# First slots of a sandwich kernel reordered: weight low parts on TensorE, second block from slot 1, third from slot 10

## Chip, cores and metric

The kernel runs on one core of a Trainium2 chip. Its time is the device time of one execution in microseconds (us): before the change the median of three runs is 1156.1 us (1156.03 to 1156.17). Where and why time goes is read from one execution that the hardware profiler recorded.

A core has five engines with a queue of instructions each, worked in order: TensorE (PE; PEld is its weight load), VectorE (DVE), ScalarE (ACT), GpSimd (POOL) and SyncE (SP), which issues nearly all of this kernel's DMAs.

## What is computed

The input is 16 sequences of 512 rows of 128 values (D = 128). Two layers follow, each with layer norms around it and an addition of its input:

```python
x = x + layernorm(attn(layernorm(x)))
x = x + layernorm(ffn(layernorm(x)))

# attn: a diagonal recurrence with 64 states, done in the reference by FFT
h = real(ifft(fft(kernel) * fft(u @ B_w.T)))
y = h @ C_w.T + D * u

# ffn: 8 experts, all of them computed, H = 128, F = 512
router_probs = softmax(x @ w_router)
gate_weights = softmax(x @ w_gating / 0.1)
g = x @ w_gate[e];  up = x @ w_up[e]
expert_out[e] = (silu(g) * up) @ w_down[e]
cw = router_probs * gate_weights
cw = cw / (sum(cw) + 1e-9)
out = sum over e of expert_out[e] * cw[e]
```

## The kernel before

**Tiling.** A block is one sequence of 512 rows (T = 512), kept with features on the 128 partitions. There are 16 blocks. A block's expert layer is 32 slots: 8 experts times 4 pieces of 128 of the 512 hidden values. Slot n makes `g` and `u` (`up`, L564 for the silu), and the piece of slot n - 4 (`LAG`) is multiplied into the expert's output (`down`). Four pieces add up in one PSUM bank, which `combine` weights with the row's `cw` and adds to the block's `acc`.

**Precision.** A float32 product is made of three products of a shorter type: `mm3` (L338, L339, L340) multiplies high by high, the weight's low part by the high part, and the weight's high part by the low part. Each weight and each moving operand so exists as a high part (a copy by ScalarE) and a low part (the difference). A weight number k is expert k // 3, and gate, up or down by k % 3. `split_w` makes the high part on ScalarE (L110) and the low part on GpSimd (L115). For the first three weights (`AHEAD`), `rest` (L682, L683) makes the difference on TensorE, as identity times the weight plus minus identity times the high part, each float32 product in two records of the profile, and ScalarE copies the result (L684).

**Slots.** The last loop writes all queues in one fixed order, slot by slot. In a slot n it emits: the high part of slot n - 1 (`split_hi`, L580, ScalarE), the six products and the silu of slot n, the down products of slot n - 4, every fourth slot `combine`, then one weight split where one is due (`n % 4 < 3`), then steps of the side work, then the low part of slot n - 1 (`split_lo`, L586, on VectorE or GpSimd) and the gate product of slot n (`gate`, L575, VectorE). Whether VectorE or GpSimd makes a low part (`lo_pool`) is decided from `busy`, three planned loads.

**Side work.** `front`, `route` and `back` are generators: everything that a block needs before its slots (layer norm, recurrence, residual, layer norm, router) and after them. Each `yield` gives a smallest distance in slots and the planned cost on VectorE, ScalarE and GpSimd; `steps` takes a step where the plan has room. `chain(b)` is `front` and `route` of block b. Chain 1 begins in slot 0, chain 2 in slot 4, chain i in slot 32 i - 67. Inside `front`, `ln_coef` makes variances on VectorE (`ve`, L281), GpSimd raises them to the power -1/2 (`rs`, L283), VectorE makes the shift (`nm`, L286). `ln_add` adds the residual (L302).

**Block 0.** Its front is written out ahead of the loop: VectorE makes the recurrence's table and state, TensorE takes state and projection (L698, L675), `residual` adds the input and takes statistics (L729), `norm` normalizes on ScalarE and VectorE (L514, L516), TensorE transposes (L752), ScalarE copies to `xh` and `xT` (L755, L756), VectorE makes `xl` (L757). `keep_warm` (L736) issues products whose result nobody reads: 9, 4 and 0 of them (`WARM`). The router's exponentials of block 0 are on ScalarE (L428, L429); those of later blocks are eight powers on GpSimd (L433).

**Buffers.** `g` has two PSUM banks and `u` three: g(n) waits for the silu of slot n - 2, and u(n) for the last reader of u(n - 3), which is `lo` where VectorE makes it and the gate product where GpSimd does. The first eight weights (`OWN`) are loaded into the rings `hi` and `lo` of the slots (five each, two of `lo` being scratch of block 0); later ones go into a ring of five, and the split of one starts the load of the fifth after it.

Of the kernel before, what the change touches and what calls it, by code (L numbers as in the profile page):

```python
# [11 lines left out]
F32 = mybir.dt.float32  # L12
F32R = mybir.dt.float32r
# [6 lines left out]
P = 128  # L20
# [6 lines left out]
NF = F // P  # L27
LAG = 4
LEAD = 67
OWN = 8  # L30
WARM = 9, 4, 0
AHEAD = 3
LN_EPS = 1e-5


# [12 lines left out]
def sandwich(ctx, tc, x, a_params, B_w, C_w, Dv, w_router, w_gating, w_gate, w_up, w_down, sines, out):  # L48
# [31 lines left out]
            nc.sync.dma_start(out=xts[b][:, k], in_=x[b].rearrange("(c p) d -> p c d", p=P)[:, k])  # L80


    spare = [hp.tile([P, F], F32R, name=f"spare{i}", tag="lo", bufs=LAG + 1).bitcast(F32) for i in range(2)]

# [51 lines left out]
    dbc = const.tile([P, D], F32, name="dbc")  # L136
    for k in range(AHEAD, OWN):
        load_w(k)
        if k == 4 and NB > 1:
            load_x(1)  # L140
            nc.sync.dma_start(out=dbc, in_=Dv.partition_broadcast(P))

# [25 lines left out]
    def bank(pl, tag, name):  # L168
        return pl.tile([P, T], F32, name=name, tag=tag)
# [176 lines left out]
    def front(b):  # L346
# [58 lines left out]
        vec.tensor_tensor(xl, xT, xh.bitcast(F32), ALU.subtract)  # L405
        blocks[b] = dict(xh=xh, xl=xl, x2=x2, xT=xT)

    def route(b):

        G2 = NT * 2  # L410
        xT = blocks[b]["xT"]
        yield 1, 0, 0, 0, "f"
        lg = ps_f.tile([P, G2, E], F32, name=f"lg{b}", tag="f")
        for c in range(NT):
            pe.matmul(  # L415
                lg[:, 2 * c : 2 * c + 2], xT[:, P * c : P * c + P], wrg.rearrange("d g e -> d (g e)"),
                start=True, stop=True,
            )
        yield 1, 0.4, 0, 0
        bc = lambda t, n: t.unsqueeze(2).broadcast_to([P, n, E])  # L420
        mx = small.tile([P, G2], F32, name="mx", bufs=2)
        vec.tensor_reduce(mx, lg, AX.X, ALU.max)
        ez = small.tile([P, G2, E], F32, name="ez", bufs=2)
        vec.tensor_tensor(ez, lg, bc(mx, G2), ALU.subtract)
        own[0] = False
        if b == 0:
            e4 = ez.rearrange("p (c g) e -> p c g e", g=2)
            act.activation(e4[:, :, 0], e4[:, :, 0], AF.Exp)  # L428
            act.activation(e4[:, :, 1], e4[:, :, 1], AF.Exp, scale=10.0)  # L429
        else:  # L430
            for i in range(G2):
                yield 1, 0, 0, 1.62
                gp.tensor_tensor(ez[:, i], bases.rearrange("p c g e -> p (c g) e")[:, i], ez[:, i], ALU.pow)  # L433
        yield 2, 0.65, 0, 0
        sm = small.tile([P, G2], F32, name="sm", bufs=2)
        vec.tensor_reduce(sm, ez, AX.X, ALU.add)
        vec.reciprocal(sm, sm)
        vec.tensor_tensor(ez, ez, bc(sm, G2), ALU.mult)
        yield 1, 0.75, 0, 0
        pr = ez.rearrange("p (c g) e -> p c g e", g=2)  # L440
        cw0 = small.tile([P, NT, E], F32, name="cw0", bufs=2)
# [78 lines left out]
    def halves(t):  # L520
        return [[t[:, 2 * h], t[:, 2 * h + 1]] for h in range(2)]
# [110 lines left out]
    def turn(k):  # L632
        for _ in range(k):
            next(rot, None)
# [60 lines left out]
    def state(c):  # L695
        k = quarter[c]
        vec.tensor_tensor(vm[:, k], v[:, k], tre[:, k], ALU.mult)
        pe.matmul(yps[c], vm[:, k], cT, start=False, stop=True)  # L698

    vec.tensor_tensor(v[:, left], bus[0], tre[:, left], ALU.mult)  # L700
    turn(2)
    scan(left, 0.0)
    turn(2)
    state(0)
    state(1)
    turn(2)
    vec.tensor_tensor(v[:, right], bus[1], tre[:, right], ALU.mult)
    lo0 = rest(0, ps_u, "u")
    lo0()
    scan(right, v[:, 2 * P - 1 : 2 * P])  # L710
    stat(0, yps[0])
    stat(1, yps[1])
    state(2)
    state(3)
    rest(1, ps_g, "g")()
    r0 = rstd(s6s[0])
    stat(2, yps[2])
    stat(3, yps[3])
    r1 = rstd(s6s[1])
    rest(2, ps_f, "f")()  # L720

# [10 lines left out]
    warm = bank(ps_g, "g", "warm")  # L732

    def keep_warm(k):
        for _ in range(k):
            pe.matmul(warm, W[0, 0][0][:, :P], W[0, 0][0], start=True, stop=True)  # L736

    keep_warm(WARM[0])
    residual(0, r0[1])
    q0 = rstd(s6s[0])  # L740
    residual(1, r1[1])
# [3 lines left out]
    xh = fe.tile([D, T], F32R, name="xh0", tag="xh", bufs=2)  # L745
    xl = fe.tile([D, T], F32R, name="xl0", tag="xl", bufs=2)
    xT = work("ft_x0")
    for h, q in enumerate((q0, q1)):
        norm(halves(xn)[h], halves(x2)[h], q[1], shift(*q), True)
        ps = bank(ps_u, "u", f"xT0{h}")[:, : 2 * P]  # L750
        for i in range(2):
            pe.transpose(ps[:, P * i : P * i + P], xn[:, 2 * h + i], ident)  # L752
        keep_warm(WARM[1 + h])
        k = slice(2 * P * h, 2 * P * h + 2 * P)
        act.copy(xh[:, k], ps)  # L755
        act.copy(xT[:, k], ps)  # L756
        vec.tensor_tensor(xl[:, k], ps, xh[:, k].bitcast(F32), ALU.subtract)  # L757
    for h, r in enumerate((r0, r1)):
        vec.scalar_tensor_tensor(x2m[:, 2 * h : 2 * h + 2], r[0][:, :, 0], -1.0, r[1], ALU.mult, ALU.mult)
    blocks[0] = dict(xh=xh, xl=xl, x2=x2, xT=xT, x2m=x2m)  # L760
    first_route = route(0)

    def first():
# [43 lines left out]
    for n in range(total + LAG):  # L807
# [8 lines left out]
        if n < total:  # L816
            up(n, *[first] * (n == 0))
        if n == 0:
            begin(n, 0, first_route, 1, routed)
            if NB > 1:  # L820
                begin(n, 1, chain(1), 1)
        if n == 3:
            act.copy(bT[0], bT32)
            gp.tensor_tensor(bT[1], bT32, bT[0].bitcast(F32), ALU.subtract)
        for i in range(NB):
            if i > 1 and n == max(4, 32 * i - LEAD):
                begin(n, i, chain(i))
        m = n - LAG
        if 0 <= m < total:
# [2 lines left out]
        if m >= 0 and m % 4 == 3:  # L832
            take((0.6, 0, 1.23), (9, 9, 9))
            combine(m // 32, m // 4 % 8)
            if m % 32 == 31 and m // 32 in accs:
                begin(n, m // 32 + 0.5, back(m // 32, accs.pop(m // 32)))
        if nsplit < 3 * E and n < total and n % 4 < 3:
            take((0, 0.5, 1.23), (9, 9, 9))
            split_next(1)
        if n < total:  # L840
# [1 line left out]
        if 0 <= n - 1 < total:  # L842
            split_lo(n - 1)
        if n < total:
            lo_pool[n] = busy[2] < busy[0] and n < total - 3
            gate(n)


# [25 lines left out]
```

## Time and profile before

| | before |
|---|---|
| median of 3 runs | 1156.1 us (1156.03 to 1156.17) |
| profiled execution's own time | 1155.96 us |
| its span, first to last instruction | 1154.1 us |
| granted TensorE clock, mean | 0.997 |
| busy: PE, DVE, ACT, POOL | 1131.5, 922.9, 698.1, 745.6 us |
| first gate product starts | 26.41 us |

In a row of the order of time, the columns are: start in us, duration in us, engine, line, operation, output <- inputs, shapes, how many, and in brackets the engine's idle time before it and what ended it. Products of TensorE overlap: one takes 0.40 us, but the next starts 0.23 us after it. A busy TensorE is therefore not always TensorE at its fastest. In a table of stretches each engine's busy time stands with its number of instructions, and after them the clock that TensorE was granted (1.00 is full speed).

### The profile page before, as it was taken

The numbers are of one execution on the slowest core, as the hardware profiler recorded it, in microseconds if no ns is written. First come the engines' busy times: TensorE is split into PE (matmuls) and PEld (weight loads), VectorE is DVE, ScalarE is ACT, GpSimd is POOL, SyncE is SP. The second block draws the span as 40 slices with busy tenths as digits, with TensorE's granted clock in tenths as the row PEclk, the third lists the DMA queues.
The fourth block names the chain that finished last, engine by engine and source line by source line (L and its number), as shares of the span: only waits on it lengthen the run. The fifth ranks groups of instructions, "written<-read, shape, count | busy, mean of one in ns | idle before, by whom it ended". The sixth has DMA issues, their size and how long they took to land.

```text
span 1154.1 us, 16183 instructions
## 1 busy us (share of the span) xinstructions
PE 1131.5 (98%) x4978; PEld 913.3 (79%) x4978; DVE 922.9 (80%) x2101; ACT 698.1 (60%) x1348; POOL 745.6 (65%) x570
## 2 busy tenths in 40 slices
PE   6899999999999999999999999999999999999997
PEld 4678788888888888888888888888888888888885
DVE  6888888887878878787887878888787887868666
ACT  3766656656566655656566565655657566565564
POOL 1679576776757766585866748577585856647442
PEclk9999999999999999999999999999999999999999
DMA  4140312203122131302212130130302202111120
GB/s 152 50 149 4 93 55 56 92 29 92 47 65 64 38 96 43 92 28 74 73 38 83 38 109 29 56 90 30 92 29 81 66 19 74 47 56 28 31 71 10
DMA packets 65894, 71.23 MB, mean 62 GB/s; under 512 B 8624, under 2 KB 50320, under 8 KB 65808
## 3 DMA queue, kind: packets, MB, share of 16 engines
q1 hardware_dynamic: 65392, 70.04, 20.0%
q8 instruction: 39, 0.64, 0.2%
q14 instruction: 47, 0.39, 0.1%
q10 hardware_dynamic: 416, 0.16, 0.1%
HBM read 54.98 MB, written 15.20 MB: 61 GB/s over the span
## 4 chain that ended last, share of the span: by engine, by line
PE 90%; DVE 4%; POOL 3%; issue 2%; ACT 0%; DMA 0%; DVEq 0%; POOLq 0%
PE g L338 10%; PE d L338 10%; PE g L340 10%; PE d L339 10%; PE uu L338 10%; PE d L340 10%; PE uu L340 10%; PE g L339 10%; PE uu L339 9%; PE yp L387 1%; POOL ez L433 1%; PE lg L415 1%; DVE x L302 0%; POOL acc L609 0%; DVE lo L586 0%
## 5 line engine op out<-in xcount | busy, mean ns | idle before, releaser
L586 POOL TENSOR_TENSOR lo<-hh,hi 128x512 fp32r<-128x512 f32 x196 | 261.9, 1336 | 155.1 <-ACT hi L580 155.0
L580 ACT CAST hi<-uu 128x512 fp32r<-128x512 f32 x316 | 185.4, 587 | 244.4 <-DVE uu L575 235.9
L564 ACT ACTIVATE sg<-g 128x512 f32<-128x512 f32 x512 | 306.7, 599 | 17.5 <-PE g L340 11.7
L575 DVE TENSOR_TENSOR uu<-sg,uu 128x512 f32<-128x512 f32 x316 | 218.7, 692 | 93.9 <-ACT sg L564 83.3
L586 DVE TENSOR_TENSOR lo<-uu,hi 128x512 fp32r<-128x512 f32 x316 | 216.9, 687 | 95.9 <-ACT hi L580 93.2
L609 POOL TENSOR_TENSOR acc<-acc,ct 128x512 f32<-128x512 f32 x109 | 142.4, 1306 | 138.9 <-DVE ct L606 89.7
L580 ACT CAST hi<-hh 128x512 fp32r<-128x512 f32 x196 | 121.6, 621 | 162.5 <-DVE hh L575 160.7
L338 PE MATMUL g<-xh,wgh 128*128 128x512 f32 x512 | 206.8, 404 | 2.4 <-ACT sg L564 1.8
L338 PE MATMUL uu<-xh,wuh 128*128 128x512 f32 x512 | 203.9, 398 | 4.3 <-DVE lo L586 4.3
L339 PE MATMUL d<-hi,wdl 128*128 128x512 f32 x512 | 203.3, 397 | 0.0
L340 PE MATMUL g<-xl,wgh 128*128 128x512 f32 x512 | 203.1, 397 | 0.0
L338 PE MATMUL d<-hi,wdh 128*128 128x512 f32 x512 | 203.0, 396 | 0.0
L340 PE MATMUL uu<-xl,wuh 128*128 128x512 f32 x512 | 201.4, 393 | 0.0
L340 PE MATMUL d<-lo,wdh 128*128 128x512 f32 x512 | 201.1, 393 | 0.0
L339 PE MATMUL g<-xh,wgl 128*128 128x512 f32 x512 | 200.8, 392 | 0.0
L339 PE MATMUL uu<-xh,wul 128*128 128x512 f32 x512 | 198.6, 388 | 0.0
L433 POOL TENSOR_TENSOR ez<-bases,ez 128x8 f32<-128x8 f32 x120 | 195.7, 1650 | 0.0
L575 DVE TENSOR_TENSOR hh<-sg,uu 128x512 f32<-128x512 f32 x196 | 133.5, 681 | 12.5 <-ACT sg L564 5.1
L338 PEld LDWEIGHTS g<-xh,wgh 128*128 128x128 f32 x512 | 96.1, 188 | 27.7 <-ACT sg L564 5.2
L338 PEld LDWEIGHTS uu<-xh,wuh 128*128 128x128 f32 x512 | 95.9, 187 | 27.8 <-DVE lo L586 6.0
L339 PEld LDWEIGHTS uu<-xh,wul 128*128 128x128 f32 x512 | 96.4, 188 | 23.8 <-POOL wul L115 0.2
L340 PEld LDWEIGHTS d<-lo,wdh 128*128 128x128 f32 x512 | 96.8, 189 | 22.9
(172 smaller groups left out, 1336.8 us busy)
## 6 DMA issues: line engine op xcount, KB each, us to landing
cwb<-scw SPq DMA_DIRECT2D x64, 512.0 KB
xt<-in_L_attn_u_dram SPq DMA_DIRECT2D x15, 256.0 KB
sco<-ob SPq DMA_DIRECT2D x60, 64.0 KB
ot<-sco SPq DMA_DIRECT2D x15, 256.0 KB
out_dram<-x SPq DMA_DIRECT2D x15, 256.0 KB
scr_u<-blk_u SPq DMA_DIRECT2D x52, 64.0 KB
ft_u<-scr_u SPq DMA_DIRECT2D x13, 256.0 KB
scr_x<-blk_x SPq DMA_DIRECT2D x52, 64.0 KB
```

The costliest lines, as they stand in the source:

```text
L338: pe.matmul(ps, w[0][:, cs], mh, start=first, stop=False)
L339: pe.matmul(ps, w[1][:, cs], mh, start=False, stop=False)
L340: pe.matmul(ps, w[0][:, cs], ml, start=False, stop=last)
L387: pe.matmul(yp[:, c], v[:, P * c : P * c + P], cT, start=True, stop=True)
L415: pe.matmul(lg[:, 2 * c : 2 * c + 2], xT[:, P * c : P * c + P], wrg.rearrange("d g e -> d (g e)"), start=True, stop=True,)
L433: gp.tensor_tensor(ez[:, i], bases.rearrange("p c g e -> p (c g) e")[:, i], ez[:, i], ALU.pow)
L564: act.activation(s, g, AF.Silu)
L575: vec.tensor_tensor(h, s, u, ALU.mult)
L580: act.copy(hi, pend[n])
L586: (gp if lo_pool[n] else vec).tensor_tensor(lo, h, hi.bitcast(F32), ALU.subtract)
L609: add = lambda: eng.tensor_tensor(acc, acc, t, ALU.add)
```

## The change

- Four weights instead of three are split by `rest`, their copies from PSUM all come at the end, and the products of the first stand ahead of the first pair of state products. Weight 3 is loaded earlier; seven weights instead of eight lie in the slots' rings, and a third scratch tile is set aside in the ring `lo`.
- The warming products are gone.
- The last normalization of block 0 is on VectorE alone, in four operations that subtract and multiply; both halves' `xl` come after both transposes. Half of the router's products stand ahead of the first gate products.
- Chain 1 begins in slot 1 and the rest of block 0's routing in slot 1 as well; chain 2 begins in slot 10. Weight splits begin in slot 3 with weight 4. In slots 0 to 3 no low part is on GpSimd.
- Block 1's exponentials are on ScalarE too, as a step with a planned cost of 1.6.

```diff
-OWN = 8
-WARM = 9, 4, 0
-AHEAD = 3
+OWN = 7
+AHEAD = 4
...
-    spare = [hp.tile([P, F], F32R, name=f"spare{i}", tag="lo", bufs=LAG + 1).bitcast(F32) for i in range(2)]
+    spare = [hp.tile([P, F], F32R, name=f"spare{i}", tag="lo", bufs=LAG + 1).bitcast(F32) for i in range(3)]
...
-        if k == 4 and NB > 1:
+        if k == OWN - 1 and NB > 1:
             load_x(1)
...
+    def logits(b):
+        return ps_f.tile([P, NT * 2, E], F32, name=f"lg{b}", tag="f")
+
+    def score(lg, xT, cs):
+        for c in cs:
             pe.matmul(
                 lg[:, 2 * c : 2 * c + 2], xT[:, P * c : P * c + P], wrg.rearrange("d g e -> d (g e)"),
                 start=True, stop=True,
             )
+
+    def route(b):
...
+        if b > 0:
+            lg = logits(b)
+            score(lg, xT, range(NT))
+        else:
+            lg = blocks[0]["lg"]
+            score(lg, xT, (2, 3))
...
-        if b == 0:
+        if b <= 1:
+            if b == 1:
+                yield 1, 0, 1.6, 0
             e4 = ez.rearrange("p (c g) e -> p c g e", g=2)
             act.activation(e4[:, :, 0], e4[:, :, 0], AF.Exp)
...
     vec.tensor_tensor(v[:, left], bus[0], tre[:, left], ALU.mult)
+    lo = [rest(0, ps_u, "u")]
     turn(2)
     scan(left, 0.0)
     turn(2)
     state(0)
     state(1)
+    lo.append(rest(1, ps_f, "f"))
     turn(2)
     vec.tensor_tensor(v[:, right], bus[1], tre[:, right], ALU.mult)
-    lo0 = rest(0, ps_u, "u")
-    lo0()
     scan(right, v[:, 2 * P - 1 : 2 * P])
     stat(0, yps[0])
     stat(1, yps[1])
     state(2)
     state(3)
-    rest(1, ps_g, "g")()
+    lo.append(rest(2, ps_g, "g"))
     r0 = rstd(s6s[0])
     stat(2, yps[2])
     stat(3, yps[3])
     r1 = rstd(s6s[1])
-    rest(2, ps_f, "f")()
+    lo.append(rest(3, ps_g, "g"))
+    for f in lo:
+        f()
...
-    keep_warm(WARM[0])
     residual(0, r0[1])
...
-    for h, q in enumerate((q0, q1)):
-        norm(halves(xn)[h], halves(x2)[h], q[1], shift(*q), True)
+    xps = []
+    lg = logits(0)
+    for h, (mv, rs) in enumerate((q0, q1)):
         ps = bank(ps_u, "u", f"xT0{h}")[:, : 2 * P]
+        xps.append(ps)
         for i in range(2):
-            pe.transpose(ps[:, P * i : P * i + P], xn[:, 2 * h + i], ident)
-        keep_warm(WARM[1 + h])
-        k = slice(2 * P * h, 2 * P * h + 2 * P)
-        act.copy(xh[:, k], ps)
-        act.copy(xT[:, k], ps)
-        vec.tensor_tensor(xl[:, k], ps, xh[:, k].bitcast(F32), ALU.subtract)
+            c = 2 * h + i
+            vec.tensor_scalar(xn[:, c], x2[:, c], mv[:, i, 0:1], rs[:, i : i + 1], ALU.subtract, ALU.mult)
+            pe.transpose(ps[:, P * i : P * i + P], xn[:, c], ident)
+        act.copy(xh[:, (left, right)[h]], ps)
+        act.copy(xT[:, (left, right)[h]], ps)
+    for h, k in enumerate((left, right)):
+        vec.tensor_tensor(xl[:, k], xps[h], xh[:, k].bitcast(F32), ALU.subtract)
+    score(lg, xT, (0, 1))
...
         if n == 0:
-            begin(n, 0, first_route, 1, routed)
-            if NB > 1:
-                begin(n, 1, chain(1), 1)
-        if n == 3:
+            begin(n + 1, 0, first_route, 1, routed)
+        if n == 1 and NB > 1:
+            begin(n, 1, chain(1), 1)
+        if n == 4:
             act.copy(bT[0], bT32)
             gp.tensor_tensor(bT[1], bT32, bT[0].bitcast(F32), ALU.subtract)
         for i in range(NB):
-            if i > 1 and n == max(4, 32 * i - LEAD):
+            if i > 1 and n == max(10, 32 * i - LEAD):
                 begin(n, i, chain(i))
...
-        if nsplit < 3 * E and n < total and n % 4 < 3:
+        if nsplit < 3 * E and n < total and (n == 3 or n > 3 and n % 4 < 3):
             take((0, 0.5, 1.23), (9, 9, 9))
             split_next(1)
...
-            lo_pool[n] = busy[2] < busy[0] and n < total - 3
+            lo_pool[n] = busy[2] < busy[0] and 4 <= n < total - 3
             gate(n)
```

More of the change, by code (lines that the diff above doesn't have):

```diff
@@ L406, in front @@
         blocks[b] = dict(xh=xh, xl=xl, x2=x2, xT=xT)
+    def logits(b):
+        return ps_f.tile([P, NT * 2, E], F32, name=f"lg{b}", tag="f")
+    def score(lg, xT, cs):
+        for c in cs:
+            pe.matmul(
+                lg[:, 2 * c : 2 * c + 2], xT[:, P * c : P * c + P], wrg.rearrange("d g e -> d (g e)"),
+                start=True, stop=True,
+            )
     def route(b):
@@ L412, in route @@
         yield 1, 0, 0, 0, "f"
[L413 to L418, printed above, removed]
+        if b > 0:
[4 more added lines that the diff above has]
+            score(lg, xT, (2, 3))
         yield 1, 0.4, 0, 0
@@ L730, in residual @@
             stat(c, x2[:, c])
[L732 to L736, printed above, removed]
-    keep_warm(WARM[0])
     residual(0, r0[1])
@@ L747, in sandwich @@
     xT = work("ft_x0")
-    for h, q in enumerate((q0, q1)):
-        norm(halves(xn)[h], halves(x2)[h], q[1], shift(*q), True)
+    xps = []
+    lg = logits(0)
+    for h, (mv, rs) in enumerate((q0, q1)):
         ps = bank(ps_u, "u", f"xT0{h}")[:, : 2 * P]
+        xps.append(ps)
         for i in range(2):
-            pe.transpose(ps[:, P * i : P * i + P], xn[:, 2 * h + i], ident)
-        keep_warm(WARM[1 + h])
-        k = slice(2 * P * h, 2 * P * h + 2 * P)
-        act.copy(xh[:, k], ps)
-        act.copy(xT[:, k], ps)
-        vec.tensor_tensor(xl[:, k], ps, xh[:, k].bitcast(F32), ALU.subtract)
-    for h, r in enumerate((r0, r1)):
-        vec.scalar_tensor_tensor(x2m[:, 2 * h : 2 * h + 2], r[0][:, :, 0], -1.0, r[1], ALU.mult, ALU.mult)
-    blocks[0] = dict(xh=xh, xl=xl, x2=x2, xT=xT, x2m=x2m)
+            c = 2 * h + i
[6 more added lines that the diff above has]
+    score(lg, xT, (0, 1))
+    for h, (mv, rs) in enumerate((r0, r1)):
+        vec.scalar_tensor_tensor(x2m[:, 2 * h : 2 * h + 2], mv[:, :, 0], -1.0, rs, ALU.mult, ALU.mult)
+    blocks[0] = dict(xh=xh, xl=xl, x2=x2, xT=xT, x2m=x2m, lg=lg)
     first_route = route(0)
```

## Prediction

> **Names.** Block 0 is worked in 32 slots. Slot n issues three gate products g(n), three up products uu(n) and, from slot 4 on, three down products d(n-4); ScalarE makes the silu sg(n) and the high part hi(n), VectorE the gate product and mostly the low part lo(n). S(n) is the start of g(n) on TensorE. Weight number k is expert k/3; k mod 3 = 0, 1, 2 is gate, up, down (wg, wu, wd).
>
> **What bounds the kernel now.** I read the stretches first. The columns are: stretch, its length, busy time of PE, PEld, DVE, ACT, POOL, granted clock, DMA share, GB/s.
>
> ```profile
> 20.00:24.00 4.00, 3.69 (x15) 2.73 (x16) 1.64 (x8) 1.48 (x4) 1.20 (x2) 1.00 0.22 66
> 24.00:28.00 4.00, 2.67 (x14) 1.50 (x12) 1.40 (x6) 1.55 (x5) 0.00 (x0) 1.00 0.00 0
> 26.40:46.40 20.00, 16.94 (x73) 12.20 (x74) 14.86 (x44) 14.75 (x31) 10.71 (x10) 1.00 0.09 28
> 46.40:80.00 33.60, 31.06 (x129) 24.08 (x128) 29.02 (x55) 22.01 (x46) 25.11 (x20) 0.95 0.43 127
> 80.00:124.00 44.00, 43.16 (x196) 34.73 (x195) 36.85 (x79) 27.87 (x54) 35.55 (x27) 1.00 0.07 24
> 124.00:1100.00 976.00, 975.88 (x4325) 794.35 (x4326) 787.73 (x1728) 596.10 (x1150) 647.99 (x481) 1.00 0.20 61
> ```
>
> From 124 us on TensorE is busy in 975.88 of 976.00 us; slots follow each other at 2.085 us (9 products of 0.2315). Nothing that is only rearranged can win there. All that can move lies ahead of 124: the time to the first product (26.41), and two holes, which the order of time shows.
>
> ```profile
> 34.96 1.01 POOL L283 TENSOR_TENSOR rs<-ve,neghalf 128x4 f32<-128x4 f32 x1
> 35.94 1.27 POOL L586 TENSOR_TENSOR lo<-hh,hi 128x512 fp32r<-128x512 f32 x1
> 36.01 1.22 DVE L286 SCALAR_TENSOR_TENSOR nm<-mv,rs 128x4 f32<-128x4 f32 x1
> 37.15 0.68 DVE L586 TENSOR_TENSOR lo<-uu,hi 128x512 fp32r<-128x512 f32 x1
> 37.88 0.50 PE L338 MATMUL uu<-xh,wuh 128*128 128x512 f32 x1 [1.88 <-DVE lo L586]
> ...
> 64.65 1.31 POOL L115 TENSOR_TENSOR wul<-raw,wuh 128x512 fp32r<-128x512 f32 x1
> 66.12 0.40 PE L339 MATMUL uu<-xh,wul 128*128 128x512 f32 x1
> ...
> 71.20 3.19 DVE L302 SCALAR_TENSOR_TENSOR x<-du,rs,xt 128x128 f32<-128x128 f32 x4
> 71.43 1.28 POOL L609 TENSOR_TENSOR acc<-acc,ct 128x512 f32<-128x512 f32 x1 [0.71 <-DVE ct L606]
> 72.68 1.31 POOL L115 TENSOR_TENSOR wul<-raw,wuh 128x512 fp32r<-128x512 f32 x1
> 74.32 0.68 DVE L586 TENSOR_TENSOR lo<-uu,hi 128x512 fp32r<-128x512 f32 x1
> 75.05 0.79 PE L338 MATMUL uu<-xh,wuh 128*128 128x512 f32 x1 [2.17 <-DVE lo L586]
> ```
>
> The reader is to see one mechanism twice. A small VectorE operation on SBUF operands (nm takes 0.15 us elsewhere) ends only when GpSimd's running operation ends (36.01 + 1.22 = 37.23, GpSimd's 35.94 + 1.27 = 37.21). Behind it in VectorE's queue stands lo, which frees the PSUM bank that uu three slots later needs. At 71.20 four such operations stood against two GpSimd operations in a row. After the second hole, products were 0.43 apart instead of 0.23 until 77.8 (granted clock 0.50 there). The middle pair is the third thing to see: the low part of expert 4's up weight ends at 65.96, and its reader starts at 66.12. There was no slack.
>
> Prices from S(n): S17 = 67.27 to S21 = 80.02 is 12.75, where four slots take 8.34: 4.4 us lost. Slot 13 lost 0.4 (58.62), slot 40 lost 0.9 (123.86). The last hole starts at slot 4.
>
> **Part 1, the way to the first product.** The x2 of the second half still needs the same VectorE chain, whose last variance ends at 21.32. After it stand today: a wait for nine warming products (20.87 to 23.50) ahead of the transposes, ScalarE's queue, and a shift coefficient at 24.78 queued behind xl, which waited 2.7 us for ScalarE. After the change the four normalizations are all on VectorE (0.35 us, some 0.23 apart) and no warming stands before the transposes. Against it: the low parts on TensorE (four passes, 0.43 apart, 1.72 us each) now stand one ahead of each pair of y products. The first starts at 13.3 and its y pair at 15.0 (was 14.00, hidden under the scan, which ends at 16.05); the second moves the other y pair from 16.69 to 17.24, and the statistics wait for it: +0.5. The chain: variance 21.8, GpSimd's power 0.70 to 22.6, last two normalizations to 23.2, transposes to 23.65, xh 23.7, first product 0.42 later as today (25.99 to 26.41): 24.1. Today it is 26.41. The third product waits for xl until 24.7 (today 27.15), and only half of the router's products stand before uu(0) (four of 0.10): uu(0) at 25.4 against 28.29: **-2.9**.
>
> Here a rule speaks against the change. "TensorE: Matmul & The Clock Gate" in the Trainium skill (Part 1: The HAM clock gate) says that the clock is halved after an idle window of about 3.4 us; the warming products kept TensorE busy. The row: 1.88 us idle before 37.88 cost no clock, 2.17 before 75.05 halved it for 2.7 us, which is earlier than a full window. Without warming, the fourth low part ends at 21.4 and gaps of 0.8, 0.5 and less follow. By the row, nothing; if the clock fell anyway, the six products up to uu(0) would cost 0.2 more each, with the router some 1.0, partly hidden under the table load. I take 0.
>
> **Part 2, slots 0 to 4.** silu, gate, high part, silu is one chain: 30.66, 31.29, 32.01, 32.54, so 1.88 a slot, more than six products (1.39). It stays. The three weight splits (ScalarE 0.5, GpSimd 1.3 each) go from slots 0 to 2, and with them the hold on VectorE; VectorE gets all of lo instead (0.62 a slot). Chain: table load ends 27.75, sg(0) 27.8, sg(1) 29.65, sg(2) 31.7, sg(3) 33.7. But weight 4 (wu of expert 1) is now split in slot 3: its ScalarE half stands behind sg(3) (34.2 to 34.8), GpSimd's ends at 36.1, and uu(4)'s second product reads it: 36.2. Behind it wait uu(4), d(0) and lo(3), which takes the buffer that d(0) frees. Today that product is at 38.22. Up to S8 both then run almost dense: 43.95 against 46.38: **-2.4**. The route arithmetic (1.6 us of VectorE) and coefficients of block 1 run in the time when GpSimd is empty.
>
> **Part 3, slots 8 to 25.** Until S12 nothing is late (S12 = 53.0, was 55.42). The splits are one slot later against their use: before, slot 12 split weights 12, 13, 14 in slots 12, 13, 14; now it is 11, 12, 13 in slots 12, 13, 14, and 12 and 13 are read in slot 16 as before. In GpSimd's queue six operations stand from slot 12 to the low part of 13 (wd 11, rs, lo, acc, wg 12, wu 13: 5 x 1.26 + 1.0 = 7.3), where four stood (60.89 to 65.96). VectorE waits in slot 10 for bu (about 50.75), so gates are 4 us behind TensorE, as today; sg(12) comes at 56.4, weight 11's split at 57.5, weight 13's low part at 65.0. uu(16) wants it at S12 + 8.34 + 0.81 (y products) + 0.93 = 63.1: **+2.0**. S17 = 66.3 (67.27).
> Slot 16: rs stands behind weight 14's low part and ends at 68.5; nm waits for it, then for lo (69.85): VectorE loses 2.9 us as at 67.27 to 69.48 today. The residual (two and two now, not four) then meets weight 16's low part until 74.9; lo(17) ends at 76.0; uu(20) starts there, against 73.8: with small waits for sg, +3.0 for slots 19 to 21. S21 = 77.8 (80.02): **-2.2**.
> Slots 20 to 24 repeat it: sg(20) at 79.3, weight 17's low part to 81.7, rs 82.7, lo 84.0, nm then; uu(23) waits from 82.7 for lo(20), 84.9: +2.2; weight 19's low part ends at 88.6, uu(24) wanted it at 87.6: +1.1. S25 = 89.9, where today it is 89.50 less 0.70 for the block 2 product that is not yet issued: 88.8. **+1.1**. Slot 28 has wd 20, ul, acc, wg 21, wu 22 and no lag left: nothing. The SP queue is no part of this: weight 3, loaded earlier, is needed at 12, x of block 1 at 29.
>
> **Part 4, block 1's exponentials.** Eight GpSimd powers (8 x 1.65 = 13.2 us) go, off the path as TensorE was full at 98 to 117. ScalarE gets two exponentials and two table loads between sg(29) and sg(30). The row for a load:
>
> ```profile
> 29.14 0.21 ACT L429 ACTIVATE ez<-ez 128x32 f32<-128x32 f32 x1
> 29.36 1.28 ACT L564 ACT_TABLE_LOAD   x1
> 30.66 0.60 ACT L564 ACTIVATE sg<-g 128x512 f32<-128x512 f32 x1
> ```
>
> "ScalarE: Activation LUTs" (What ACT_TABLE_LOAD costs) gives 1283 ns for the load and some 1380 ns more to drain, 2.66 for a switch. The row shows 1.28 and the silu 0.02 after it: no second part. By the row sg(30) is 2 x 1.28 + 0.4 = 3.0 late, and g(32), two slots on, allows about 3.0: **+0.3** (0 to 0.6). By the page it would be 5.7 late: +2.7. I take the row. The late hole of slot 40 may go with the powers or stay: **-0.4**. The third block from slot 10 instead of 4 only frees VectorE early; its end, slot 64, is far.
>
> **Sum.** +1.1 + 0.3 - 0.4 = +1.0 on the profiled execution's own 1155.96: 1157.0; the median lies 0.1 above it: **1157.1**. So 2.4 won at the head is given back between slots 16 and 25, while the old hole of 4.4 reappears as smaller ones.
>
> **Rivals.** (a) The holes don't come back. For it: a residual in pairs gives lo its turn; three splits are gone from slots 0 to 2; nm at 48.98 passed in 0.15 when GpSimd was idle. Against: three of four nm here stood 1.2 us. Then -2.4 - 4.8 and up to 2.5 for the late weights: 1149 to 1152.5, about 1151. (b) Slower: the half clock. Two holes of part 3 last 1.9 and 2.2 us, at the edge of the 1.88 that did nothing and the 2.17 that halved it; the price at 75.05 was six products of 0.2 plus the change over, 1.3 to 1.4. It decides from one such hole (1158.5); with both, 1159.9. (c) The order does nothing to the head: if the first product waits for something not seen, part 1's 2.9 is less; it would need ScalarE's four low-part copies (last to 22.05) to hold xh at 22.8. Unlikely; 1158 to 1159, counted with (b).
>
> **Numbers.** A measurement of this kernel can tell about 0.2% (2.3 us) from no change: 1153.8 to 1158.4. Forecast 0.48 (own range 1154 to 1159: faster 0.02, same 0.38, slower 0.08); (a) 0.23 (faster 0.20, same 0.03); (b) and (c) 0.29 (same 0.04, slower 0.25). Together faster 0.22, same 0.45, slower 0.33. Range 1151 to 1160.5: the likely part of (a) below, both half clocks above.
>
> **To check in the profile of the changed kernel.** First product at 24.1 and uu(0) at 25.4 (part 1; half clock there would show in products 0.43 apart); uu(4)'s second product at 36.2 released by GpSimd's wul (part 2); S8 at 44, S12 at 53; a wait of uu(16) on wul near 63 to 65, nm of about 1.2 us ahead of lo, waits at uu(20), uu(23), uu(24) (part 3); two loads of 1.28 and g(32) at most a little late (part 4). It would be wrong if those waits are absent, if they come with a clock of 0.5, or if slots after 32 open.

## The result: slower by 12.6 us

The changed kernel takes 1168.73 us (median; 1168.47 to 1169.02), the kernel before 1156.13 us: 1.0106 of it, with a 95% interval of 1.0088 to 1.0123. The forecast was 1157.1, and its range ended at 1160.5. Its profiled execution has a span of 1167.1 us (1154.1 before).

The stretches of the changed kernel come first, with the columns of the prediction's first view (stretch, length, busy time of PE, PEld, DVE, ACT and POOL, granted clock, DMA share, GB/s).

```profile
24.00:28.00 4.00, 3.96 (x15) 3.10 (x15) 1.35 (x6) 1.29 (x5) 0.00 (x0) 0.60 0.00 1
34.00:38.00 4.00, 1.64 (x6) 0.81 (x5) 3.39 (x13) 3.40 (x8) 1.29 (x1) 1.00 0.00 0
38.00:42.00 4.00, 4.00 (x13) 3.13 (x12) 1.82 (x3) 3.20 (x8) 1.78 (x3) 0.57 0.05 8
80.00:84.00 4.00, 4.00 (x14) 3.10 (x12) 3.34 (x12) 2.67 (x6) 1.06 (x1) 0.64 0.37 111
124.00:194.00 70.00, 69.92 (x311) 56.63 (x310) 60.67 (x137) 42.68 (x87) 47.16 (x36) 1.00 0.20 57
194.00:218.00 24.00, 19.11 (x70) 14.44 (x69) 14.19 (x28) 12.45 (x26) 8.11 (x7) 0.86 0.40 118
218.00:1100.00 882.00, 882.00 (x3912) 718.06 (x3911) 712.80 (x1563) 538.60 (x1034) 587.69 (x436) 1.00 0.19 58
```

Three things are to be seen. The clock is at 0.60 in 24 to 28, at 0.57 in 38 to 42 and at 0.64 in 80 to 84, where it had been 1.00. Behind 124, where TensorE had next to no idle time before, 4.9 us of it lie in 194 to 218, and the clock is 0.86 there. From 218 on TensorE is full again. So all of the loss lies ahead of 218 us.

The order of time on TensorE names the larger waits of the changed kernel (start, length, operation, and in brackets the idle time before it and what ended it).

```profile
35.92 0.49 PE L337 MATMUL uu<-xh,wuh 128*128 128x512 f32 x1 [1.49 <-ACT wuh L109]
37.29 0.50 PE L338 MATMUL uu<-xh,wul 128*128 128x512 f32 x1 [0.87 <-POOL wul L114]
...
78.65 0.47 PE L337 MATMUL uu<-xh,wuh 128*128 128x512 f32 x1 [2.00 <-DVE lo L597]
...
110.67 0.50 PE L337 MATMUL g<-xh,wgh 128*128 128x512 f32 x1 [1.48 <-ACT sg L575]
...
210.64 0.80 PE L337 MATMUL uu<-xh,wuh 128*128 128x512 f32 x1 [4.17 <-DVE lo L597]
```

The first pair (slot 4) waits for the late split of weight 4, as forecast. The wait at 78.65 is the old hole of slot 20, about 2 us in both kernels. The two below, in slots 32 and 75, were not in the sum at this size (0.3 was set for slot 32, nothing for slot 75). The account, from the starts of the g products (S(n), the prediction's names):

| | S(0) | S(0) to S(8) | to S(32) | to S(72) | to S(76) |
|---|---|---|---|---|---|
| before | 26.41 | 19.97 | 59.90 | 86.93 | 8.35 |
| changed | 24.59 | 22.21 | 63.87 | 88.13 | 14.57 |
| difference | -1.82 | +2.24 | +3.97 | +1.20 | +6.22 |

The sum at S(76) is +11.8; a last microsecond of half clock lies just behind it. Of the +1.20, 0.8 is no loss: block 2's y products stand ahead of slot 32 in the kernel before and behind it in the changed one, so the loss made by slot 32 is rather 4.8 than 4.0. Half of the loss is made in four slots of block 2, more than 40 slots behind the last edited one. The start of the first product differs between executions of one head (all work ahead of slot 0) by more than 1 us: 26.41 in the kernel before and 28.19 in E3, which has the same head. Profiles are therefore compared below from S(0) on.

What the 4.17 us wait for, along the queue of SP (SPq rows are DMA issues) and VectorE, in order of time, in the changed kernel:

```profile
198.10 2.84 SPq L465 DMA_DIRECT2D scw<-cwT  x4
201.03 1.83 SPq L487 DMA_DIRECT2D sco<-ob  x4
204.34 0.34 SPq L492 DMA_DIRECT2D ot<-sco  x1
204.78 0.37 SPq L473 DMA_DIRECT2D cwb<-scw  x1
208.70 0.69 DVE L612 TENSOR_TENSOR acc<-d,cwb 128x512 f32<-128x512 f32 x1 [4.77 <-DMA cwb<-scw]
```

and in the kernel before:

```profile
187.89 2.83 SPq L454 DMA_DIRECT2D scw<-cwT  x4
191.98 0.33 SPq L462 DMA_DIRECT2D cwb<-scw  x1
197.18 0.69 DVE L601 TENSOR_TENSOR acc<-d,cwb 128x512 f32<-128x512 f32 x1
197.70 1.88 SPq L476 DMA_DIRECT2D sco<-ob  x4
```

The router's weights of block 2 go to DRAM (scw) and come back spread over all partitions (cwb). Before, the load was issued ahead of block 1's result (sco, ot) and 5.2 us before its use. Now it stands behind it. ot can't be issued until sco has landed, and cwb, which has nothing to do with either, waits behind ot in the same queue. VectorE then stands 4.77 us at the combine, with lo behind it and uu behind lo.

The reason is two slots of the plan. The planner decides from planned costs alone, so its slots can be worked out from the kernel: it ends block 2's routing in slot 68 before and in slot 70 now, and the load follows one slot later: 69 or 71. In slot 71 block 1's result (begun in slot 69, rank 1.5) has its turn too, and comes ahead of rank 2 (a chain's rank is its block number, and a block's result has half more).

The same working out, edit by edit, names the edit that takes the two slots: block 1's start in slot 1 instead of 0. With the exponentials of block 1 on ScalarE as the only edit the routing ends in slot 68, with that start added in 70. In the changed kernel with the third block from slot 4 it ends in 70, with block 1 put back to slot 0 in 68. This is a reading of the plan; no run tests that edit alone.

### The profile page after: what moved, and what is told of

Read it like the earlier page. It is cut to its first block, busy times and chain, and to the rows that moved or that the text cites. A ratio compares the mean times of both kernels' runs of the same rounds, so it can differ in the third digit from the quotient of the medians.

```text
span 1167.1 us, 16167 instructions
## 1 busy us (share of the span) xinstructions
PE 1138.3 (98%) x4969; PEld 916.0 (78%) x4969; DVE 920.8 (79%) x2099; ACT 702.6 (60%) x1351; POOL 732.6 (63%) x563
## 4 chain that ended last, share of the span: by engine, by line
PE 89%; DVE 5%; issue 2%; ACT 1%; POOL 1%; DMA 1%; SPq 1%; DVEq 0%; ACTq 0%; POOLq 0%
PE g L337 10%; PE g L339 9%; PE d L337 9%; PE d L338 9%; PE uu L337 9%; PE d L339 9%; PE uu L339 9%; PE g L338 9%; PE uu L338 9%; DVE uu L586 1%; PE yp L386 1%; PE lg L412 1%; DVE lo L597 1%; ACT hi L591 1%; DVE hh L586 1%
## 5 line engine op out<-in xcount | busy, mean ns | idle before, releaser
L444 POOL TENSOR_TENSOR ez<-bases,ez 128x8 f32<-128x8 f32 x112 | 182.9, 1651 | 0.0
L339 PEld LDWEIGHTS uu<-xl,wuh 128*128 128x128 f32 x512 | 96.5, 189 | 24.0
```

The source lines that it names most:

```text
L339: pe.matmul(ps, w[0][:, cs], ml, start=False, stop=last)
```

## The experiments

Times are medians; ratios are to the kernel before, measured beside each.

| run | us | ratio, 95% interval |
|---|---|---|
| E1 weights loaded first | 1163.44 | 1.0056 (1.0039 to 1.0072) |
| E2 third block from slot 4 | 1168.50 | 1.0101 (1.0086 to 1.0116) |
| E3 before, weights loaded late | 1163.89 | 1.0062 (1.0047 to 1.0077) |
| E4 splits from slot 2 | 1164.70 | 1.0068 (1.0053 to 1.0083) |
| E5 powers in pairs | 1163.82 | 1.0062 (1.0047 to 1.0077) |
| E6 warming back | 1167.19 | 1.0090 (1.0073 to 1.0107) |
| E7 before, exponentials alone | 1155.64 | 0.9992 (0.9982 to 1.0001) |
| E8 head alone | 1156.26 | 0.9994 (0.9984 to 1.0003) |
| E9 two causes undone | 1159.38 | 1.0026 (1.0017 to 1.0036) |
| E10 four causes undone | 1157.58 | 1.0006 (0.9996 to 1.0015) |
| E11 head and exponentials | 1154.96 | 0.9985 (0.9976 to 0.9994) |
| E12 low parts ahead | 1153.68 | 0.9974 (0.9964 to 0.9985) |
| E13 changed kernel again | 1168.61 | 1.0102 (1.0088 to 1.0116) |
| E14 warming back, again | 1167.29 | 1.0094 (1.0080 to 1.0108) |
| E15 low parts ahead twice | 1156.30 | 0.9990 (0.9981 to 0.9999) |

### E1 to E3: the queue, the start, and the same fault in the kernel before

E1, in the changed kernel:

```diff
         for i in range(4):
-            yield max(1, 32 * b + 8 * i + 2 - now[0]), 0, 0, 0
+            if i or b != 2:
+                yield max(1, 32 * b + 8 * i + 2 - now[0]), 0, 0, 0
```

> The changed kernel with one line moved: the first load of block 2's router weights (cwb) is issued in the same step as the stores it reads back (scw), so it stands in SP's queue ahead of the stores and the load of block 1's result (sco, ot) and no longer behind them. Theory Q (SP's queue): the 4.17 us wait in slot 75 and the half clock after it are there because cwb was issued at 204.78 behind ot, which waited for sco. With the load ahead it is issued near 201.0, when scw has landed, and lands near 203.7, where VectorE began to wait at 203.9: the hole is gone or under 0.5 us, granted clock 1.00 at 206 to 216, 6.5 to 7 us less, 1162 us. Theory S (the third block starts too late, in slot 10): its routing is late whatever the queue does; cwT is at 197.8 as before, and most of the hole stays: 1166 to 1169.

Order of time in E1, SP's queue and VectorE:

```profile
196.59 2.84 SPq L465 DMA_DIRECT2D scw<-cwT  x4
200.60 0.32 SPq L474 DMA_DIRECT2D cwb<-scw  x1
204.76 0.69 DVE L613 TENSOR_TENSOR acc<-d,cwb 128x512 f32<-128x512 f32 x1 [2.35 <-DMA cwb<-scw]
```

1163.44 is 5.3 us under the changed kernel (expected 6.5 to 7). The order in the queue was the larger part; but VectorE's wait is 2.35, not gone. I had taken 2.7 us from issue to landing, and it was 4.2 (200.60 to 204.76). With that, cwT itself comes too late, and the queue can't mend it.

E2, in the changed kernel: `n == max(10, 32 * i - LEAD)` becomes `n == max(4, 32 * i - LEAD)`.

> The changed kernel with the third block begun in slot 4 again. Theory S (late start of the third block makes its router weights late): routing ends earlier, the wait in slot 75 is gone, 7 us less, about 1162. Theory Q (SP's queue, at a routing that is two slots later because of the planner's other changes): the planner still ends the routing of block 2 in slot 70, since the steps in between fill up the six slots, and cwb still follows sco and ot on SP: the hole of about 4 us and the half clock stay, 1167 to 1170, the slots up to 25 moved by up to 1 either way.

Order of time in E2, SP's queue and VectorE:

```profile
197.81 1.84 SPq L327 DMA_DIRECT2D scr_x<-blk_x  x4
201.14 0.34 SPq L332 DMA_DIRECT2D ft_x<-scr_x  x1
201.57 1.83 SPq L487 DMA_DIRECT2D sco<-ob  x4
205.15 0.34 SPq L492 DMA_DIRECT2D ot<-sco  x1
205.53 0.43 SPq L473 DMA_DIRECT2D cwb<-scw  x1
209.53 0.69 DVE L612 TENSOR_TENSOR acc<-d,cwb 128x512 f32<-128x512 f32 x1 [9.11 <-DMA cwb<-scw]
```

The start slot is not the cause: the plan still ends the routing in slot 70, and the time is unchanged. But the hole did not stay at 4 us. cwb now stands behind two pairs of store and load back, VectorE waits 9.11 us and TensorE 7.94. That E2 isn't slower is due to 2.9 us won on the way to S(72), counted from S(0): g(32) no longer waits (below), and slots 16 to 25 are tighter.

E3, in the kernel before: the first of the four loads for block 2 gets `max(3, ...)` in place of `max(1, ...)`, so that it is issued in slot 71.

> The kernel before, with one thing taken over from the changed one: block 2's first router weights (cwb) are issued in slot 71, behind the stores and the load of block 1's result, and not in slot 69 ahead of them. Theory Q: block 2's first combine waits for them, TensorE gets a hole of 3 to 4 us near slot 75 and 6 us at half clock after it: 1162 to 1164. Theory S, or any theory in which TensorE's stop at slot 75 has another cause: the weights still come in time, 1156.

Order of time in E3, SP's queue, VectorE and TensorE:

```profile
201.25 0.34 SPq L481 DMA_DIRECT2D ot<-sco  x1
201.63 0.91 SPq L462 DMA_DIRECT2D cwb<-scw  x2
205.75 0.69 DVE L601 TENSOR_TENSOR acc<-d,cwb 128x512 f32<-128x512 f32 x1 [6.69 <-DMA cwb<-scw]
...
208.34 0.79 PE L338 MATMUL g<-xh,wgh 128*128 128x512 f32 x1 [4.81 <-ACT sg L564]
```

One load issued two slots later, behind ot, makes the kernel before 7.3 us slower (1163.89 against 1156.62; by the interval 5.4 to 8.9). S(72) to S(76) takes 13.32 us instead of 8.35, and the rest is half clock behind it (0.50 in 206 to 212). This settles the cause and size of the largest term without any other part of the change.

### E4: splits from slot 2

```diff
-        if nsplit < 3 * E and n < total and (n == 3 or n > 3 and n % 4 < 3):
+        if nsplit < 3 * E and n < total and (n in (2, 3) or n > 3 and n % 4 < 3):
```

> The changed kernel with the weight splits one slot earlier (weight 4 in slot 2, 5 in slot 3, and so on, so that each has the same distance to its first use as in the kernel before). Theory W (late low parts): the waits of uu(4) at 34.4 to 38.2 (2.4 us) shrink to under 1 us, with it the half clock at 38.7 to 41.5 goes (1.3), S8 comes at 43 to 44 and not at 46.8, the waits of slots 16 and 24 on GpSimd's low parts (1.0, 0.3, 0.7) are gone, and 3 to 5 us stay at the end: 1164 to 1166. Rival V (VectorE and GpSimd are the bound of slots 8 to 25, whatever the lead): the time won by slot 8 is lost again by slot 25 in waits for lo, as it was in the kernel before: 1167.5 to 1169.

TensorE in E4, order of time:

```profile
35.09 0.50 PE L338 MATMUL uu<-xh,wul 128*128 128x512 f32 x1 [0.64 <-POOL wul L114]
...
37.95 0.50 PE L337 MATMUL uu<-xh,wuh 128*128 128x512 f32 x1 [0.73 <-DVE lo L597]
```

4.0 us are back. S(0) to S(8) is 20.16 instead of 22.21, since two short waits replace 1.49 and 0.87 and the clock stays at 1.00 in 38 to 42. S(8) to S(32) is 0.9 shorter, all of it behind slot 25 (S(8) to S(25) is 45.67, as against 45.56), and S(32) to S(72) 1.0. Rival V fell in what it forecast, since what was won by slot 8 was not lost again; but the earlier splits gave slots 8 to 25 nothing: waits for lo (0.67, 0.90 and 1.90 in slots 13, 19 and 20) stand where waits for weights were. The hole at slot 75 was as large as ever (4.25).

### E5: powers in pairs

```diff
-                yield 1, 0, 0, 1.62
+                if b != 2 or i % 2 == 0:
+                    yield 1, 0, 0, 1.62
```

> The changed kernel with block 2's eight powers on GpSimd issued two to a slot, so that its routing ends four slots earlier (slot 66 and not 70); nothing else is moved. The run with the load put first kept 2.35 of VectorE's wait because cwT itself came late (196.2, the load then issued at 200.6). Theory QT (queue and a late cwT together are all of the 7 us): the hole at slot 75, the half clock after it and the 0.5 of sg at slot 72 go, 6.5 to 7 us less, 1161.6 to 1162.3. Rival R (pairs of powers hold VectorE's small operations, or the rest of the hole has another cause): 1163.5 or more, with holes of over 0.5 near slots 58 to 66 or still at 75.

VectorE and TensorE in E5, order of time:

```profile
185.66 0.22 DVE L448 TENSOR_REDUCE sm<-ez 128x8 f32<-128x64 f32 x1 [4.69 <-POOL ez L445]
...
189.13 0.50 PE L337 MATMUL g<-xh,wgh 128*128 128x512 f32 x1 [2.87 <-ACT sg L576]
```

With the routing done in slot 66, S(72) to S(76) is 8.34: the hole of slot 75 and its half clock are gone. But two powers a slot are more than GpSimd had room for, VectorE stood 4.69 us at the sum of the powers, and 2.87 us of hole (with half clock behind it) came in at slot 67. Rival R was right about the time, QT about the hole.

### E6, E13, E14: the warming products

Four products ahead of the first pair of transposes and one ahead of the second (`keep_warm((4, 1)[h])`); E13 is the changed kernel as it is.

> The changed kernel with five warming products on TensorE put back (four ahead of the first two transposes, one ahead of the last two), into gaps of 0.88 and 0.35 us. Theory H (the missing warming costs the clock, and the silu chain hides most of it): granted clock 1.00 at 24 to 28, products 0.23 apart, router products 0.5 and not 0.87; but the first silu waits for router, exponentials and table load, so only about 0.6 arrive in slot 8 and at the end: 1168.1. Rival H2 (all is on the path: nine products of 0.2 more and the router's 0.4): 1166.3 to 1167. Rival H3 (the lost clock has nothing to do with the gaps): still 0.5 at 24 to 28, 1168.7.

> The changed kernel as it is, beside the next run on the same chip, so that its time with and without warming can be compared there. It also shows whether the half clock at 24 to 28 comes in each execution: with the same code ahead of the first product the three profiles whose first product came at 23.6 to 23.7 had it at 1.00, the four at 24.2 to 24.8 at about half. Theory F (it depends on where the gap ahead of the first product falls in time): 1.00 if the first product starts before 23.8, about 0.5 if after 24.1. Theory E (the two groups differ by chance of something else): any mix. Time 1168.5 either way, or 0.6 less where the clock stays.

> The same with the five warming products. Theory H (the clock is lost without them and the silu chain hides most): 0.3 to 0.8 less than the unchanged one beside it, clock 1.00 at 24 to 28 wherever the first product starts. Rival H2 (all of the slower products counts): 1.5 to 2.5 less. Rival H3 (no effect on time, since in many executions the clock stays at 1.00 anyway): within 0.3.

E13 and E14 each have one line for the stretch 24 to 28, in this order:

```profile
24.00:28.00 4.00, 4.00 (x12) 3.28 (x13) 1.01 (x5) 1.34 (x4) 0.00 (x0) 0.50 0.00 0
```

```profile
24.00:28.00 4.00, 3.79 (x17) 2.54 (x16) 1.01 (x5) 2.05 (x6) 0.00 (x0) 1.00 0.00 0
```

Their first products start at 23.94 and 24.06, so they can be laid side by side: S(0) to S(8) is 22.35 without warming and 21.58 with it, 0.8 us. The times differ by 1.3 (E6 and the first run of the changed kernel: 1.5), with intervals that overlap; they don't tell 0.8 from 1.5. E6 alone could not show the cause: without warming, E1, E5 and E9 had a clock of 1.00 there too. All profiles fit one order. Without warming, first products at 23.61, 23.66 and 23.70 kept the clock, and those at 23.94, 24.23, 24.27, 24.59 and 24.83 lost it (0.50 to 0.68 in 24 to 28). With warming, all six from 23.62 to 24.54 kept it. The gaps ahead of the product are the same in all (0.88 and 0.35 us); where they fall in time differs by 0.2 to 1.2 us. That the position decides is what the order suggests; no run moved the gap alone.

### E7, E8, E11: parts on their own in the kernel before

E7 takes only the branch `if b <= 1` with its step of 1.6. E8 keeps the new head and undoes all rules of the slots. E11 is E8 with the exponentials and the warming of E6.

> The kernel before with block 1's exponentials on ScalarE, that part alone. Theory X (the two table loads open a hole two slots later, as g(32) waited 1.48 in the changed kernel): a wait of 1 to 1.8 for the silu near slot 30 to 32, and the 0.71 of slot 40 gone or not: 1156.8 to 1158. Theory P (as predicted: 0.3 more, 0.4 less): 1156.0 to 1156.5. In both the routing of block 2 still ends in slot 68 and its weights are in time.

> The way to the first product alone: low parts of four weights on TensorE, no warming, normalizations on VectorE, half of the router's products; but weights split from slot 0 in three slots of four, block 1 begun in slot 0, block 2 in slot 4, powers of block 1 on GpSimd and the low parts of slots 0 to 3 shared with GpSimd, as in the kernel before. Theory L (the lead of 1.8 at the first product lasts if the slots behind it are as before): 1154.0 to 1155. Rival G (it is lost again in slots 0 to 25, since half clock and silu chain take 0.6 and GpSimd and VectorE set those slots): 1156 to 1157.5.

> The head alone with block 1's exponentials on ScalarE and the five warming products; splits from slot 0, blocks 1 and 2 begun in slots 0 and 4 and low parts shared in slots 0 to 3, as in the kernel before. The head alone kept 0.6 of its 1.6; its clock was 0.68 and 0.65 in 24 to 34. Theory L (the clock took the lead's other half): clock 1.00 there and the full 1.6, with 0.5 to 1 of the exponentials alone: 1154.0 to 1154.8. Rival G (GpSimd and VectorE set slots 4 to 25 and take it back): 1155.5 to 1156.5.

E7 is not slower; theory X fell. The exponentials alone cost nothing, and S(72) comes 0.5 earlier. So the wait of g(32) in the changed kernel needs something else. ScalarE and VectorE around it, in the changed kernel:

```profile
104.39 2.13 DVE L380 TENSOR_TENSOR_SCAN v<-v,zero 128x512 f32<-128x512 f32 x1
...
105.01 1.28 ACT L439 ACT_TABLE_LOAD   x1
...
107.41 0.68 DVE L586 TENSOR_TENSOR uu<-sg,uu 128x512 f32<-128x512 f32 x1
...
108.12 0.59 ACT L591 CAST hi<-uu 128x512 fp32r<-128x512 f32 x1 [1.46 <-DVE uu L586]
...
108.72 1.28 ACT L575 ACT_TABLE_LOAD   x1
...
110.02 0.60 ACT L575 ACTIVATE sg<-g 128x512 f32<-128x512 f32 x1
```

and in E2, whose third block starts in slot 4:

```profile
100.02 1.37 DVE L380 TENSOR_TENSOR_SCAN v<-v,zero 128x512 f32<-128x512 f32 x1
...
103.73 1.28 ACT L439 ACT_TABLE_LOAD   x1
...
105.28 0.57 ACT L591 CAST hi<-uu 128x512 fp32r<-128x512 f32 x1
...
105.87 1.28 ACT L575 ACT_TABLE_LOAD   x1
```

Two table loads are there both times. With the scan of the third block 3.7 us ahead of them, the high part follows the exponentials at once and the loads start 2.1 us apart. With the scan beside them (2.13 us long, against 1.37) the gate product behind it in VectorE's queue started at 107.41 and the high part at 108.12, ScalarE idled 1.46 between the loads, and g(32) waited 1.48. Here the start in slot 10 does cost.

E8 starts the first product 1.6 earlier than the kernel before, and its time can't be told from it (rival G); at S(72) 0.7 was left. S(0) to S(8) is as long as before (20.16), with a clock of 0.68 in 24 to 28; part of the lead went between S(32) and S(72), 88.07 against 86.93, in no wait above 0.5 us; and at 350.29, in a later block, TensorE waits 1.05 us that the kernel before doesn't have. E11, with the clock at 1.00, is 1.5 in a thousand faster than the kernel before: between its two expectations.

### E9 and E10: the causes taken out together

E9 is E4's and E5's edits, with block 2's sums two slots later (routing in slot 68). E10 adds E6's warming and E2's start.

> The changed kernel with two causes taken out together: weights split from slot 2, and block 2's powers issued in pairs with their sums two slots later (routing ends in slot 68, so that its weights are loaded ahead of block 1's result, and VectorE doesn't wait for the powers as it did for 4.7 us in the run with pairs alone). Theory A (the two causes are separate and add up): 4.0 of the splits and 7.0 of the router's weights: 1157.5 to 1158.5, no hole of over 1 us behind slot 40, about 2 us of holes left at slots 16 to 32. Rival B (VectorE's room is what is short, so a hole taken away comes back a few slots later, as 2.9 us did at slot 68): 1160 or more.

> As the run with two causes undone, and also five warming products put back and the third block begun in slot 4 (so that its scan doesn't meet the two table loads of slot 29, and g(32) doesn't wait). Theory A (adds up): 0.6 of the clock and 1.5 to 2 of slot 32 more: 1155.3 to 1156.3, what is left of the change being the lead of 1.8 at the first product against the hole at slot 20, which both kernels have. Rival B (holes come back elsewhere): 1158 or more.

E9 fell between theory A and rival B, 9.3 us under the changed kernel where 10.2 to 11.2 were expected. S(72) to S(76) is 8.38, but a wait of 1.15 for a silu stands in slot 70. E10 can't be told from the kernel before: 1.0006, 11.2 us under the changed kernel, and between its two expectations. The four causes hold most of the loss; but the first product's lead is not kept either, as waits of 1.73 (slot 20, lo), 1.58 (slot 23, lo), 0.67 (slot 32) and 1.62 (slot 69, silu) are left or new.

### E12 and E15: the hole that both kernels had

E12 is E11 with this edit; E15 has `early` also for slots 2 to 4.

```diff
+        early = 16 <= n <= 24
+        if early:
+            split_lo(n - 1)
         if n < total:
             steps(n)
-        if 0 <= n - 1 < total:
+        if 0 <= n - 1 < total and not early:
             split_lo(n - 1)
```

> As head and exponentials, and in slots 16 to 24 the low part lo of the slot before is put into VectorE's queue ahead of the side work (nm, residual, statistics) and no longer behind it. Theory N (the hole of 2.2 us at slot 20, which both kernels have, is there because lo stands behind nm and the residual, which GpSimd's operations hold): that hole and its half clock shrink, 2 to 3 us less than the run beside it, 1151.5 to 1153. Rival O (the side work then delays the gate and by it the high parts and silu, and the hole comes back): within 1 us of it, or slower.

> As the run with the low parts ahead in slots 16 to 24, and also in slots 2 to 4, where nm (1.22 us instead of 0.15) stands ahead of lo and uu(4) waits 1.88 us. Theory N (the same mechanism): the wait of uu(4) falls to under 0.9, 1 to 1.5 us less, 1152.2 to 1152.8. Rival O (the small operations of block 0's routing then come late and router weights or gates with them): no gain, 1153.5 or more.

E11, VectorE and TensorE in order of time:

```profile
68.46 3.20 DVE L301 SCALAR_TENSOR_TENSOR x<-du,rs,xt 128x128 f32<-128x128 f32 x4
...
71.58 0.68 DVE L597 TENSOR_TENSOR lo<-uu,hi 128x512 fp32r<-128x512 f32 x1
...
72.31 0.79 PE L337 MATMUL uu<-xh,wuh 128*128 128x512 f32 x1 [2.16 <-DVE lo L597]
```

E12, the same stretch, with ScalarE:

```profile
68.09 0.69 DVE L597 TENSOR_TENSOR lo<-uu,hi 128x512 fp32r<-128x512 f32 x1 [0.62 <-ACT hi L591]
...
68.70 2.18 DVE L301 SCALAR_TENSOR_TENSOR x<-du,rs,xt 128x128 f32<-128x128 f32 x4
...
71.51 0.62 ACT L591 CAST hi<-hh 128x512 fp32r<-128x512 f32 x1 [2.45 <-DVE hh L586]
...
72.67 0.50 PE L337 MATMUL g<-xh,wgh 128*128 128x512 f32 x1 [1.72 <-ACT sg L575]
```

lo comes 3.5 us earlier in the profile (0.4 of it is an earlier start) and no uu waits for it, but now the gate stands behind the four residual operations, and g(20) waits 1.72 for its silu. The clock stays at 1.00 in 64 to 80 (0.79 in E11), which is most of the gain: 2.0 us from S(0) to S(72), 1.3 in the time (2 to 3 were expected), where the intervals of the two overlap. 1153.68 us is the fastest kernel of the study, 0.26% under the kernel before. In E15 the same order in slots 2 to 4 turned a wait of 1.88 for lo into one of 2.64 for the silu, with the clock at 0.57 behind it: rival O, and 2.6 us worse.

## Why the prediction was wrong

**The step that failed** is the last sentence of part 4: that the third block from slot 10 "only frees VectorE early; its end, slot 64, is far". With it everything behind slot 40 stood at nothing in the sum, and part 3 set the queue of SP aside ("The SP queue is no part of this") after a look at weight 3 and x of block 1 only. I did not follow block 2 to its end. It ended in slot 68 before, for a use in slot 73; under the change it ends in slot 70, and the load of the router's weights changed places with another block's result in SP's queue. This is 7 of the 12.6 us (E3: 7.3). It isn't the third block's start that takes the two slots (E2: slot 70), nor the exponentials alone (E7: slot 68); by the plan it is block 1's start in slot 1, to which the prediction gave no cost. The sign that I had named for being wrong, "if slots after 32 open", is what came.

**Part 1.** The first product came at 24.59 (forecast 24.1), and at 23.6 to 24.8 in the other profiles with this head: right within what a start differs by. "I take 0" for the clock was wrong in the profiled execution: products 0.43 apart from 24.59, uu(0) at 26.63 instead of 25.4. The price I named for it, 1.0, partly hidden, was near: 0.8 (E13, E14). "TensorE: Matmul & The Clock Gate" in the Trainium skill (Part 1: The HAM clock gate) gives an idle window of about 3.4 us as the condition, and says that the window runs freely. Gaps of 0.88 and 0.35 us were enough here, so the first doesn't hold as a bound; the second agrees with a gap that costs the clock in five profiles and not in three.

**Part 2.** uu(4)'s second product was named with its releaser and came at 37.29 (forecast 36.2); that was right. What I left out is that waits of 1.49 and 0.87 us cost the clock again: 0.57 in 38 to 42. S(8) came at 46.80 and not at 43.95, and the 2.4 us that the sum won there were gone.

**Part 3** held in its sum and in part in its terms. S(8) to S(25) was forecast as 45.95 (43.95 to 89.9) and measured as 45.56 (46.80 to 92.36); before it was 43.12. The late low parts of slots 16 and 24 and the wait for lo at uu(20) (2.00) came where they were named, though the wait in slot 16 fell on g(16) (1.02) more than on uu(16) (0.28). The waits at uu(23) and uu(24) were 0.44 and 0.66, where 2.2 and 1.1 were forecast, and behind uu(20) the clock halved, which the sum had left out: that the two errors nearly cancel is luck. The splits' old distance is not the lever of these slots either, since E4 leaves them as long as they are; what it brings back lies in part 2 (2.05) and behind slot 25. The third block's start in slot 4 (E2) brings back 1.2 of them. What holds the rest stays open; with all rules of the slots undone (E8) they take 43.05.

**Part 4's own sum.** The table load took 1.28 with the silu 0.02 behind it (108.72 + 1.28 = 110.00, then 110.02), so the row was the right choice over the page "ScalarE: Activation LUTs" in the Trainium skill (What ACT_TABLE_LOAD costs), which counts 1380 ns more for each switch. Alone the exponentials cost nothing, as summed (E7). In the changed kernel g(32) waited 1.48 instead of 0.3, with the scan of the third block beside the loads (E2 and E7, without it there, have no such wait).

**Rivals.** (a) did not come: the holes are back. (b), slower by a half clock in the holes, had the right sign and a true mechanism. It was placed at slots 20 and 23; it came behind slot 20 (0.64 in 80 to 84), not behind slot 23, and also at 0, 4 and 75. (c) fell: the first product is earlier, by 1.8 in the two profiles. None of the three named a DMA queue.

## What to carry to other kernels

Where a planner packs side work, a change in any slot moves the end of every chain behind it: look up the slot in which each chain ends, before and after, against the slot that needs it, and the order in which the DMAs of different chains then meet in one queue. A load behind another chain's store and load back waits for a round trip that isn't its own. And a wait taken off one engine's queue by reordering is worth what the next wait in line leaves of it: E1, E2, E5, E9 and E12 all gave back part of their gain.

## What the runs showed of the hardware

- The load of the router's weights took 3.9 to 4.2 us from issue to use (204.78 to 208.70, 200.60 to 204.76, 205.53 to 209.53), though its issue is 0.3 to 0.4 us on SP. A deadline has to be counted from there.
- The clock fell behind 1.49 and 0.87 us of idle 0.5 us apart (38 to 42 at 0.57). It fell behind 1.83 us in one piece in E2 (uu(20) at 77.44; 0.73 in 80 to 84), but not behind 1.88 us in the kernel before (uu(4) at 37.88; 1.00 in 38 to 42), and it stayed in three profiles and fell in five behind the same gaps of 0.88 and 0.35. The length of a gap alone doesn't tell.
- The half clock lasted some 3 us behind the short gaps (products 0.43 apart from 24.6 to 28.0) and longer behind the hole of 4.17 (0.67 in 212 to 218).
